# Stopping VectorE more often for GpSimd's gathers in a graph kernel that sorts neighbours

## The chip, the cores and the metric

The kernel runs on one core of one Trainium2 chip. The metric is the time of one execution on the device, in microseconds (us). A core has five engines that run their own instruction queues at the same time: TensorE (PE in the profile, PEld for its weight loads), VectorE (DVE), ScalarE (ACT), GpSimd (POOL) and SyncE (SP, which here issues plain DMA transfers). They wait for one another through semaphores. Each queue is executed in the order in which it was written.

## What is computed

There are 16 graphs of 1024 nodes; a node has 64 features. Two layers follow one another, each with a residual and a layer norm. The first removes a part of the edges, takes for each node and feature a weighted sum of three quantiles over the neighbours that remain, and puts that through a small network. The second multiplies the adjacency with the features and applies another small network. Cut to what matters:

```python
x, adj, nodemask          # (16, 1024, 64), (16, 1024, 1024), (16, 1024)

def layer_0(x, adj, mask, W1, b1, W2, b2):
    adj_d = dilate(adj, mask)          # drops every skip-th neighbour, symmetrically
    agg = 0                            # per node and feature, over its neighbours:
    for tau, wt in zip([0.25, 0.5, 0.75], [0.25, 0.5, 0.25]):
        agg += wt * quantile(sorted neighbours, tau)   # linear interpolation
    h = relu((x + agg) @ W1 + b1)
    return (h @ W2 + b2) * mask[..., None]

def layer_1(x, adj, W1, b1, W2, b2):
    messages = einsum('bij,bjh->bih', adj, x)
    return tanh(concatenate([x, messages]) @ W1 + b1) @ W2 + b2

x = layernorm(x + layer_0(x, adj, nodemask, ...))
x = layernorm(x + layer_1(x, adj, ...))
```

The edge part of the second layer does not enter the result.

## The kernel before

The 16 graphs are worked through in nine groups: one graph, seven times two graphs, and one graph (`sizes`). For each graph three kinds of work follow one another.

*Finding* (`find`, from line 495) reads the adjacency, transposes it on TensorE (`nb`, `p_nb`, `nb_t`, lines 545 to 549), counts and ranks the neighbours (`p_cnt`, `p_m`, `s`, `p_rank`, `gone`, lines 564 to 602), applies the removal (`p_stay`, `valid`, line 625), orders the nodes by their number of neighbours (`kinds`, `low`, `places`, `p_srt`, `x_q`) and writes for every node a list of its neighbours' numbers (`word`, `bits`, `codes`, `index`). At each step ScalarE or VectorE takes TensorE's result out of PSUM.

*Gathering and sorting.* The ordered nodes lie in tiles of 128. A group of two graphs has 16 tiles, worked through in eight pairs (`group.pairs`); a group of one has four pairs. For a pair, `gather` issues one indirect DMA for each position of the list (line 876): it fetches for 128 nodes one neighbour's 64 features[...]. A tile of a pair, `g`, holds as many cells of 64 columns as there are positions, twice over. Four such buffers form a ring (`RING`): the fifth pair can be gathered when the first is sorted and added up. `sort` then orders each feature's neighbours with a network of minima and maxima. Each step is a `compare`: one VectorE tensor_tensor on one or more cells of `g` (their places given by a box of start, two steps and two counts), with 64 columns a cell. All of VectorE's instructions that go through the helper `Counted` stand in the profile under line 443. When a list is sorted, `weigh` has ScalarE multiply the wanted cells in place by their weights (line 907), and `add_up` has TensorE add them (`p_agg`, lines 924 and 928), after which the buffer is free.

*Closing* (`close`) returns the sums to the nodes' own order (`back`, `parts`, `p_g`, line 965), runs both small networks and layer norms (`p_h`, `p_y`, `p_x`, `p_adj`, `p_msg`, `p_z`, `p_d`), and writes the result.

The order of all this is fixed when the program is written. `Counted` keeps an account of VectorE's time in estimated microseconds (`vector.now`). The steps of finding and closing (`Steps`) have due times on that account, and before each compare the function `around` issues those that are due. So VectorE's queue is a mixture of compares and of steps of other graphs, and each step holds up the compares behind it until its input is there.

*Stops.* `Counted` also keeps a due time for a stop. Before an instruction with two tensor inputs, if the due time has passed, it issues a `tensor_reduce` of two columns into `pause` (line 437), an instruction with one input whose result nobody uses. It reads two columns of the cell that the fourth compare back wrote (`vector.written`), and the next stop is due 1.32 us later (`GATHER`). An instruction that has not two tensor inputs and reaches the due time moves it on in the same way.

Of the kernel before, what the change touches and what calls it, by code (L numbers as in the profile page):

```python
# [17 lines left out]
ALU = mybir.AluOpType  # L18
AX = mybir.AxisListType
# [96 lines left out]
@lru_cache(None)  # L116
def network(n, least):

    def step(layer, at, way):
        at, lows, highs = dict(at), [], []
        for i, j, low, high in layer:
            ci, cj = i + n * at[i], j + n * at[j]
            at[i] ^= low and way != "high"
            at[j] ^= high and way != "low"
            oi, oj = i + n * at[i], j + n * at[j]
            if low:
                lows.append((ci, cj, oi))  # L130
            if high:
                highs.append((ci, cj, oj))
        pair = [(ALU.min, lows), (ALU.max, highs)]
        done = []
        for op, vectors in pair[::-1] if way == "high" else pair:
            done += [(op, box) for box in boxes(tuple(sorted(vectors)))] if vectors else []
        return done, at

    states = [(0, {k: 0 for k in range(n)}, [])]
    for layer in layers_of(n, least):  # L140
        found = {}
        for _, at, done in states:
            for way in ("both", "low", "high"):
                more, to = step(layer, at, way)
                key = tuple(to.values())
                if key not in found or len(found[key][2]) > len(done) + len(more):
                    found[key] = (len(done) + len(more), to, done + more)
        states = sorted(found.values(), key=lambda s: s[0])[:12]
    places = needed(n, least)
    ends = [(s[0] + len(boxes(tuple((k + n * s[1][k], i) for i, k in enumerate(places)))), j)  # L150
            for j, s in enumerate(states)]
    _, at, done = states[min(ends)[1]]
    found = [k + n * at[k] for k in places]
    return done, boxes(tuple((c, i) for i, c in enumerate(found))), found
# [3 lines left out]
def kernel(  # L158
# [15 lines left out]
    nc = tc.nc  # L174
    B, N, C = x.shape
# [201 lines left out]
    for t in range(NT):  # L377
# [5 lines left out]
                             ap=[in_block.ap[0], [NT + 1, NT]]), 1.0)  # L383
# [12 lines left out]
    CLOSING, CLOSING_LAST = 0.8, 60.0  # L396
    TURNING = 40.0
    RING = 4
    GATHER = 1.32
    pause = const.tile([P, 1], F32, name="pause")  # L400

    def block(t):
# [5 lines left out]
    class Counted:  # L408
# [9 lines left out]
        def __getattr__(self, name):  # L418
            def size_of(x):
                n = 1  # L420
                for step, size in x.ap[1:]:
                    n *= size
                return n

            def issue(out, *args, **more):
                inputs = [a for a in args if isinstance(a, bass.AP)]
                n = max([size_of(out)] + [size_of(a) for a in inputs])
                each, more_us = 0.00104, 0.0
                if name in ("tensor_scalar", "tensor_copy"):
                    each = 0.00032 if out.dtype in (BF16, F16) and inputs[0].dtype in (BF16, F16) else 0.00053  # L430
                if name == "match_replace" or "accum_out" in more:
                    more_us = 0.07
                us = 0.067 + more_us + n * each
                two = name in ("tensor_tensor", "tensor_add", "tensor_sub", "tensor_mul",
                               "scalar_tensor_tensor")
                if two and self.now >= self.due and len(self.written) >= 4:
                    nc.vector.tensor_reduce(pause, self.written[-4], AX.X, ALU.max)  # L437
                    self.due = self.now + GATHER
                    self.now += 0.065
                elif not two and self.now + us >= self.due:  # L440
                    self.due = max(self.now, self.due) + GATHER
                self.now += us
                return getattr(nc.vector, name)(out, *args, **more)  # L443
            return issue

    vector = Counted()
# [381 lines left out]
            to.add(0.2, weigh)  # L828
        return to

    def cells(g, box, which, width):

        start, (d1, n1), (d2, n2) = box
        return bass.AP(tensor=g.tensor, offset=g.offset + start[which] * width,
                       ap=[g.ap[0], [d2[which] * width, n2], [d1[which] * width, n1], [1, width]])

    def few(G):

# [56 lines left out]
    def sort(group, k, g):  # L895

        tile_k, (u, v) = TILES[group.G][k], divmod(k, group.G)
        steps, _, where = network(*tile_k)
        todo = []

        def compare(op, box):
            vector.tensor_tensor(cells(g, box, 2, C), cells(g, box, 0, C), cells(g, box, 1, C),
                                    op=op)
            vector.written = vector.written[-3:] + [g[:, box[0][2], :2]]

        def weigh(cell, place):
            nc.scalar.mul(g[:, cell], g[:, cell], group.weights[:, v, u, place:place + 1])  # L907

        for op, box in steps:
            todo.append((compare, (op, box)))  # L910
        return todo, [(weigh, (cell, place)) for place, cell in enumerate(where)]
# [452 lines left out]
    with (  # L1364
# [25 lines left out]
        with tc.For_i(0, C, 1) as c:  # L1390
# [21 lines left out]
            for t in range(NT):  # L1412
                for h in range(2):
# [3 lines left out]
                    for k in range(NT):  # L1417
                        nc.tensor.matmul(p[:, :HALF], val_t[:, k, t * P:(t + 1) * P],
                                         before[:, k, js].rearrange("p q j -> p (q j)"),
                                         start=(k == 0), stop=(k == NT - 1))  # L1420
                    w = dense.tile([P, HALF], F32, name="w", bufs=2)
# [49 lines left out]
```

## Time and profile before

| | us |
|---|---|
| median of three runs | 3934.4 |
| lowest and highest of the three | 3887.4, 4052.7 |
| profiled execution | 3815.4 |
| its span | 3813.7 |
| VectorE busy / GpSimd busy / TensorE busy | 2329.5 / 2104.7 / 1942.5 |

The profile is of one execution, and all parts below are parts of its span. In a row of the costliest groups stand the line, the engine, the operation, the tiles written and read, and the number of instructions; after the first bar the time that they were busy and the mean of one in nanoseconds; after the second the idle time of the engine just before them, and what ended most of it. VectorE's instructions overlap by some 80 ns, so their busy times add up to more than the time that they take. "issue" is time in which an engine waited for nothing that the profile shows. A timeline row begins with the start and the duration in us. A row of the stage table has the stretch, its length, the busy time of PE, PEld, DVE, ACT and POOL, each with its number of instructions, the granted TensorE clock, the DMA share and GB/s. TensorE's clock was granted at 0.709 of full speed on average.

### The profile page before, as it was taken

The numbers are of one execution on the slowest core, as the hardware profiler recorded it, in microseconds if no ns is written. First come the engines' busy times: TensorE is split into PE (matmuls) and PEld (weight loads), VectorE is DVE, ScalarE is ACT, GpSimd is POOL, SyncE is SP. The second block draws the span as 40 slices with busy tenths as digits, with TensorE's granted clock in tenths as the row PEclk, the third lists the DMA queues.
The fourth block names the chain that finished last, engine by engine and source line by source line (L and its number), as shares of the span: only waits on it lengthen the run. The fifth ranks groups of instructions, "written<-read, shape, count | busy, mean of one in ns | idle before, by whom it ended". The sixth has DMA issues, their size and how long they took to land.

```text
span 3813.7 us, 37663 instructions
## 1 busy us (share of the span) xinstructions
PE 1942.5 (51%) x10312; PEld 1070.0 (28%) x10312; DVE 2329.5 (61%) x9225; ACT 1324.3 (35%) x2945; POOL 2104.7 (55%) x1943
## 2 busy tenths in 40 slices
PE   5206523731565442963439635674336645674376
PEld 3103312420333221532224323332113323242133
DVE  4208624991598635885268844877248765768653
ACT  3204423431443332542325323544224334134123
POOL 1760346077654766167572677447571576757750
PEclk9556756765788666875669756786667866777578
DMA  2101111121212201222022212032021321242111
GB/s 99 20 19 48 58 50 32 65 52 24 64 44 87 66 18 62 82 66 43 17 67 93 67 30 65 23 105 64 18 66 28 94 58 26 60 117 62 20 47 29
DMA packets 268306, 205.67 MB, mean 54 GB/s; under 512 B 92634, under 2 KB 225290, under 8 KB 268086
## 3 DMA queue, kind: packets, MB, share of 16 engines
q1 hardware_dynamic: 207382, 147.10, 12.1%
q0 software_dynamic: 59744, 55.90, 7.5%
q8 instruction: 83, 1.36, 0.2%
q14 instruction: 137, 1.12, 0.1%
q10 hardware_dynamic: 960, 0.18, 0.0%
HBM read 203.97 MB, written 4.19 MB: 55 GB/s over the span
## 4 chain that ended last, share of the span: by engine, by line
PE 30%; another core or an unknown queue 25%; DVE 22%; ACT 9%; issue 8%; POOL 4%; DMA 1%; SPq 0%; ACTq 0%; DVEq 0%; POOLq 0%
DVE g L443 12%; PE p_msg L1144 5%; POOL g L876 4%; PE p_srt L687 3%; PE p_g L965 3%; PE p_adj L1135 2%; PE p_rank L596 2%; PE p_rank L593 2%; PE p_agg L924 2%; PE p_cnt L564 1%; PE p_nb L545 1%; ACT nb_t L549 1%; ACT g L907 1%; DVE codes L443 1%
## 5 line engine op out<-in xcount | busy, mean ns | idle before, releaser
L876 POOL DMA_INDIRECT g<-in_x_dram,index x1859 | 2075.7, 1117 | 1470.3 <-issue 560.1
L443 DVE TENSOR_TENSOR g<-g 128x128 f32<-128x128 f32 (+7 forms) x4982 | 1581.3, 373 | 199.7 <-remote 93.7
L545 PE MATMUL p_nb<-ident_h,nb 128*128 128x128 bf16 x1024 | 107.9, 280 | 649.6 <-DVE nb L443 261.9
L437 DVE TENSOR_REDUCE pause<-g 128x1 f32<-128x2 f32 x1021 | 148.5, 145 | 272.2 <-ACT g L907 240.5
L907 ACT ACTIVATE g<-g,weights 128x64 f32<-128x64 f32 x1006 | 260.0, 338 | 102.7 <-DVE g L443 84.3
L965 PE MATMUL p_g<-back,parts 128*64 128x512 bf16 x720 | 197.9, 425 | 186.6 <-DVE back L443 138.5
L443 DVE TENSOR_SCALAR gone<-gone,s 128x1024 bf16<-128x1024 f16 x128 | 64.3, 503 | 362.8 <-ACT gone L598 222.8
L598 ACT ACTIVATE gone<-p_rank,s 128x1024 f16<-128x1024 f32 x128 | 141.5, 1112 | 402.2 <-remote 303.2
L545 PEld LDWEIGHTS <-nb 128*128 128x128 bf16 x1024 | 92.6, 130 | 670.4 <-issue 489.9
L1144 PE MATMUL p_msg<-adj_t,x 128*64 128x512 f32 x416 | 232.3, 661 | 65.9 <-issue 30.4
L593 PE MATMUL p_rank<-after,blocks 8*128 8x512 bf16 x256 | 121.4, 474 | 282.0 <-ACT gone L598 147.5
L549 ACT ACTIVATE nb_t<-p_nb 128x1024 bf16<-128x1024 bf16 x124 | 122.1, 1023 | 375.0 <-remote 247.9
L924 PE MATMUL p_agg<-g,ident 128*128 128x128 f32 x918 | 161.6, 332 | 131.3 <-ACT g L907 83.7
L687 PE MATMUL p_srt<-pay,perm 128*128 128x323 bf16 x1024 | 187.0, 320 | 52.0 <-DVE x_q L443 29.4
L625 ACT ACTIVATE valid<-p_stay 128x1024 bf16<-128x1024 f32 x128 | 130.4, 1019 | 173.5 <-remote 95.0
L924 PEld LDWEIGHTS p_agg<-g,ident 128*128 128x128 f32 x918 | 143.0, 236 | 151.9 <-ACT g L907 96.4
L1137 ACT COPY adj_t<-p_adj 128x512 f32<-128x512 f32 x208 | 117.4, 584 | 162.6 <-PE p_adj L1135 79.0
L596 PEld LDWEIGHTS <-nb_t 128*128 128x128 bf16 x1024 | 70.6, 111 | 365.1 <-issue 365.1
L618 PE MATMUL p_stay<-nb,ident_h 128*128 128x512 bf16 x256 | 115.1, 450 | 105.8 <-ACT valid L625 56.3
L965 PEld LDWEIGHTS <-parts 128*64 128x64 bf16 x720 | 80.0, 119 | 280.1 <-issue 178.8
L517 ACT ACTIVATE nb<-a 128x1024 bf16<-128x1024 f32 x124 | 125.4, 1051 | 67.2 <-remote 27.1
L1135 PE MATMUL p_adj<-ident,a_block 128*128 128x128 f32 x832 | 138.6, 300 | 14.3 <-ACT z_t L1156 11.6
(188 smaller groups left out, 3054.9 us busy)
## 6 DMA issues: line engine op xcount, KB each, us to landing
a<-in_adj_dram SPq DMA_DIRECT2D x64, 1024.0 KB
a_block<-in_adj_dram SPq DMA_DIRECT2D x208, 256.0 KB
g<-in_x_dram,index POOLq DMA_INDIRECT x1859
a_ahead<-in_adj_dram SPq DMA_DIRECT2D x48, 256.0 KB
x_f<-in_x_dram SPq DMA_DIRECT2D x16, 256.0 KB
out_dram<-o SPq DMA_DIRECT2D x16, 256.0 KB
x_c<-in_x_dram SPq DMA_DIRECT2D x15, 256.0 KB
few<-index SPq DMA_DIRECT2D x45, 0.0 KB
```

The lines of the kernel that those rows point to most:

```text
L437: nc.vector.tensor_reduce(pause, self.written[-4], AX.X, ALU.max)
L443: return getattr(nc.vector, name)(out, *args, **more)
L545: nc.tensor.transpose(p[:, t], v["nb"][:, t, block(j)], ident_h)
L549: nc.scalar.activation(v["nb_t"][:, j], p.rearrange("p t c -> p (t c)"), AF.Relu)
L593: nc.tensor.matmul(p[:, half_of(h)], v["blocks"][:, block(t)], after[:, half_of(h)], start=True, stop=False, skip_group_check=True)
L687: nc.tensor.matmul(p[:, k, :PAY], v["perm"][:, t, block(2 * at + k)], pay[:, t], start=(t == 0), stop=False, skip_group_check=True)
L876: nc.gpsimd.indirect_dma_start(out=part[:, j, :], out_offset=None, in_=x_rows, in_offset=bass.IndirectOffsetOnAxis(ap=group.index[:, v, sl ...
L907: nc.scalar.mul(g[:, cell], g[:, cell], group.weights[:, v, u, place:place + 1])
L924: nc.tensor.matmul(p, ident, it, start=(k == 0), stop=(k == most - 1), skip_group_check=True)
L965: nc.tensor.matmul(v["p_g"][h][:C, :HALF], v["parts"][:, k, q], m[:, half_of(h)], start=(k == 0 and v["start"]), stop=(k == 2 and q == v[" ...
L1135: nc.tensor.transpose(p[:, block(t)], m[:, t], ident)
L1144: nc.tensor.matmul(v["p_msg"][C:2 * C, :HALF], v["x1"][:, j, :], adj_t, start=(j == 0), stop=(j == NT - 1))
```

## The change

Three things change, all in the stops and the compares.

1. The interval of the stops becomes 0.44 us (`STOP`) instead of 1.32 us.
2. A compare is split by columns where a stop falls due within it: the first part has as many columns as fit before the due time (an even number), and the next part begins with a stop. Neither part may be shorter than 0.1 us by the account (`SPLIT`); otherwise the compare stays whole.
3. `written` holds the buffer and the cell of up to eight compares. When `weigh` begins on a list, that list's entries are taken out, so that a stop reads no cell that ScalarE multiplies. A stop reads the fourth entry from the end, or the oldest if there are fewer; with none there is no stop.

```diff
-    GATHER = 1.32
+    STOP = 0.44
+    SPLIT = 0.1
...
-                if two and self.now >= self.due and len(self.written) >= 4:
-                    nc.vector.tensor_reduce(pause, self.written[-4], AX.X, ALU.max)
-                    self.due = self.now + GATHER
+                if two and self.now >= self.due and self.written:
+                    g, cell = self.written[-4:][0]
+                    nc.vector.tensor_reduce(pause, g[:, cell, :2], AX.X, ALU.max)
+                    self.due = self.now + STOP
                     self.now += 0.065
                 elif not two and self.now + us >= self.due:
-                    self.due = max(self.now, self.due) + GATHER
+                    self.due = max(self.now, self.due) + STOP
...
-    def cells(g, box, which, width):
+    def cells(g, box, which, width, columns):
 
         start, (d1, n1), (d2, n2) = box
-        return bass.AP(tensor=g.tensor, offset=g.offset + start[which] * width,
-                       ap=[g.ap[0], [d2[which] * width, n2], [d1[which] * width, n1], [1, width]])
+        return bass.AP(tensor=g.tensor, offset=g.offset + start[which] * width + columns.start,
+                       ap=[g.ap[0], [d2[which] * width, n2], [d1[which] * width, n1],
+                           [1, columns.stop - columns.start]])
...
         def compare(op, box):
-            vector.tensor_tensor(cells(g, box, 2, C), cells(g, box, 0, C), cells(g, box, 1, C),
-                                    op=op)
-            vector.written = vector.written[-3:] + [g[:, box[0][2], :2]]
+
+            us = 0.00104 * C * box[1][1] * box[2][1]
+            done = 0
+            while done < C:
+
+                due = vector.due if vector.now < vector.due else vector.now + 0.065 + STOP
+                many = 2 * int(C * (due - vector.now - 0.067) / us / 2 + 0.5)
+                to = C if many * us / C < SPLIT or (C - done - many) * us / C < SPLIT else done + many
+                vector.tensor_tensor(*[cells(g, box, which, C, slice(done, to)) for which in (2, 0, 1)],
+                                     op=op)
+                done = to
+            vector.written = vector.written[-7:] + [(g, box[0][2])]
 
         def weigh(cell, place):
+            vector.written = [w for w in vector.written if w[0] is not g]
             nc.scalar.mul(g[:, cell], g[:, cell], group.weights[:, v, u, place:place + 1])
```

## The prediction

> **What bounds the kernel now.** I read the page first (busy shares, the chain that ended last, the costliest groups), then the groups kept apart by shape, the waits of VectorE's stops, timelines of a few microseconds, and the stage table.
>
> ```profile
> PE 1942.5 (51%) x10312; PEld 1070.0 (28%) x10312; DVE 2329.5 (61%) x9225; ACT 1324.3 (35%) x2945; POOL 2104.7 (55%) x1943
> ...
> PE 30%; another core or an unknown queue 25%; DVE 22%; ACT 9%; issue 8%; POOL 4%; DMA 1%; SPq 0%; ACTq 0%; DVEq 0%; POOLq 0%
> DVE g L443 12%; PE p_msg L1144 5%; POOL g L876 4%; PE p_srt L687 3%; PE p_g L965 3%; PE p_adj L1135 2%; PE p_rank L596 2%; PE p_rank L593 2%; PE p_agg L924 2%; PE p_cnt L564 1%; PE p_nb L545 1%; ACT nb_t L549 1%; ACT g L907 1%; DVE codes L443 1%
> ...
> L876 POOL DMA_INDIRECT g<-in_x_dram,index x1859 | 2075.7, 1117 | 1470.3 <-issue 560.1
> ...
> L437 DVE TENSOR_REDUCE pause<-g 128x1 f32<-128x2 f32 x1021 | 148.5, 145 | 272.2 <-ACT g L907 240.5
> ```
>
> No engine is full. Of the chain, compares (DVE g) hold 12% and gathers (POOL g) only 4%. The 25% of "another core or an unknown queue" is neither: one core runs. Its long pieces are ScalarE waiting for TensorE answers. Two such waits from the timeline, ScalarE alone:
>
> ```profile
> 918.46 1.02 ACT L549 ACTIVATE nb_t<-p_nb 128x1024 bf16<-128x1024 bf16 x1 [17.88 <-remote]
> 940.87 1.02 ACT L549 ACTIVATE nb_t<-p_nb 128x1024 bf16<-128x1024 bf16 x1 [21.38 <-remote]
> ```
>
> Eight transposes of about 1 us together are answered 18 and 21 us late. All through this stretch gathers run one per 1.30 us with no break and VectorE is nearly idle; where VectorE is full and gathers come 1.5 us apart, such delays are under 4 us. I do not know the mechanism; I use the pattern.
>
> The stage table shows how a group of two graphs (here 2126 to 2606 us) is made up; each busy time is followed by its count:
>
> ```profile
> 2126.00:2206.00 80.00, 51.23 (x227) 26.19 (x225) 70.15 (x274) 32.82 (x99) 55.51 (x47) 0.80 0.27 71
> 2206.00:2348.00 142.00, 66.42 (x344) 40.55 (x345) 57.54 (x225) 47.76 (x113) 104.85 (x96) 0.59 0.17 39
> 2348.00:2505.00 157.00, 102.69 (x632) 57.79 (x632) 120.86 (x474) 63.82 (x127) 70.86 (x61) 0.78 0.23 73
> ```
>
> The third number is VectorE. In the first and last stage it leads, in the middle one it waits for late answers. Gathers are early for the sorts there: pair 0 of the group that sorts from 2348 us had landed by 2291 us. GpSimd, done with four pairs, then waits for a free buffer (p_agg L928, 331.4 us in 7 waits over the run).
>
> **What the change adds to VectorE.** The order of the built program counts 1021 stops before and 2818 after; compare instructions go from 4982 to 5278; all other VectorE instructions, GpSimd's gathers and SyncE's DMAs keep their numbers. A stop's price is the time from its start to the next start:
>
> ```profile
> 1095.88 3.71 DVE L443 TENSOR_TENSOR g<-g 128x384 f32<-128x384 f32 x12
> 1096.35 4.12 POOL L876 DMA_INDIRECT g<-in_x_dram,index  x1 [0.30 <-issue]
> ...
> 1100.10 0.14 DVE L437 TENSOR_REDUCE pause<-g 128x1 f32<-128x2 f32 x1
> 1100.16 0.28 DVE L443 TENSOR_TENSOR g<-g 128x128 f32<-128x128 f32 x1
> ```
>
> It is 0.065 us here (median over all 1021), so 1797 more cost 116 us. A split costs the fixed part of a compare: two of 64 columns instead of one of 128.
>
> ```profile
> L443 DVE TENSOR_TENSOR g<-g 128x128 f32<-128x128 f32 x1091 | 284.1, 283 | 59.3 <-remote 41.2 <-DVE g L443 15.4 <-issue 2.7
> ...
> L443 DVE TENSOR_TENSOR g<-g 128x64 f32<-128x64 f32 x1207 | 232.6, 216 | 11.2 <-DVE g L443 7.3 <-issue 2.9 <-DVE pause L437 0.7
> ```
>
> 67 ns per 64 columns and 135 ns start to start for 64 leave 68 ns fixed; 296 splits make 20 us. Together 136 us, or 11% on compares that take 1192 us start to start. How much is on the path? Compares hold 12% of the chain, 458 us, 38% of their 1192: 0.38 x 136 = 52 us. The stage table says the same from another side: nine groups of 15 us each, a third of which falls in the waiting stage. I take +55 us, bounds +20 and +136. The cover is the waits for ScalarE and TensorE inside the interleaved steps; without it all 136 us show.
>
> **What stops buy.** Behind twelve compares without an opening, the gather above took 4.12 us instead of 0.997. Over the trace 664 of 1859 gathers took over 1.03 us, 224 us of excess, and 331 of them ended 935 to 965 ns after a stop's start: a gather needs one opening near its beginning, and then runs through whatever VectorE does. With a stop due every 0.44 us a full VectorE opens within about 0.5 us instead of the present median of 1.56 us between stops, so I halve the excess: 112 us of GpSimd time. Its share on the path is small: POOL and DMA hold 5% of the chain, 190 us of 2652 us of gathering (7%), so 8 us. To it comes the tail (3123 to 3566 us), where gathers run nearly without a wait and the last group's sort waits for them (30.2 us, one wait): half of some 25 us of excess there. I take -15 us, bounds 0 and -112.
>
> Here the Trainium skill speaks against the change twice (SBUF — State Buffer, section "Who interferes with whom"). It says that the two engines' shared port is an exclusive lock held for a whole instruction, the loser blocking fully, and it infers that a two-input compare takes only the read side and leaves descriptor writing free. By the inference stops buy nothing: the gain is 0 and the sum rises by 15. By the lock a compare issued after a stop would wait out the gather, up to 0.95 us for each of 2818 stops. The trace differs from both: the 4.12 us gather was held by compares, and the compare at 1100.16 started 0.065 us after its stop, with the gather still running. I follow the rows.
>
> **What no stop waits for any more.** 240.5 us of stops waiting for ScalarE's multiplications, 22 waits:
>
> ```profile
>   ACT g L907: 240.5, 22
> ```
>
> That is the row of line 437. One of these waits in VectorE's timeline:
>
> ```profile
> 2175.92 2.97 DVE L443 TENSOR_TENSOR g<-g 128x64 f32<-128x64 f32 x9
> 2184.32 0.15 DVE L437 TENSOR_REDUCE pause<-g 128x1 f32<-128x2 f32 x1 [5.44 <-ACT g L907]
> ```
>
> They fall in two kinds. Thirteen of 2 to 9 us stand in full compare stretches, as here, with 4 to 84 us of ready work behind them: together 73 us, of which I credit 45, because the next wait (1.2 us at 2205, then 8.61 us for p_d at 2229) takes up a part. The long ones (74.05 us at 954, 33.4 at 1904, 16.1, 13.9, 12.9) are followed by only 1 to 4 us of work and then by the graph search's own wait (s for p_m at 957.8; low for valid at 2343), late next in their place. I credit 5 us. Sum -50 us, bounds 0 and -240. The stop that remains reads a compare made up to four earlier, at times the last one: 39.2 us in 54 waits of VectorE for itself bounds that at +10 us, by its nearest row; a gain is excluded, since a wait only adds. I take 0.
>
> **Order.** Each sort counts as longer in the planner, so search and closing steps come earlier, by about 0.5% of all compare columns, about 6 us. With them moves every DMA they issue: GpSimd's queue keeps its order, but on SyncE's the loads of `few` and `a_block` change places here and there. In the timeline at 861 us SyncE takes 0.58 to 0.84 us to issue one such DMA, so a set of twenty put ahead of an `a_block` load delays it by some 14 us, or frees it by as much; GpSimd waits for `few_x`, TensorE's p_adj and ScalarE behind it for `a_block`. Both ways, I take 0, with 15 us a group at the very most.
>
> Sum: 55 - 15 - 50 = -10 us on 3813.7 us of span (3815.4 us with what lies around it): 0.3%, which is nothing. The profiled execution was 119 us below the median of three, 3934.4 us; from that median I predict **3930 us**.
>
> **Rivals.**
> *Slower: TensorE answers later.* Stretched gathers may be what lets TensorE through: with stops, gathers in full stretches come nearer to 1.35 us apart instead of 1.5 to 1.6, and the late answers of the middle stage start some 20 us earlier in each group. At about 5 us an answer and three answers a group that waits on them, eight groups give +120 us, and with the stop cost uncovered (+80 over my 55) +200: 4040 to 4130 us. For it: answers 10 us late already at 1.38 us spacing (2604 to 2632 us). Against it: in full stretches at 1.43 us there were none. It decides if the spacing in full stretches falls under about 1.4 us.
> *Faster: the stops' waits were the path.* If the 73 us count in full, 50 of the long 167 us as well, and half of the halved gather excess (56 us), the sum is 55 - 73 - 50 - 56 = -124 us: 3810 us. For it: the search's transposes wait for VectorE's nb (261.9 us in 9 waits), which lies behind those stretches. Against: the short work behind the long waits.
> *It doesn't do what it says:* the first compare of a pair finds no cell to stop on, and stops where no gather runs buy nothing. The cost stays, the gain goes: +55 - 50 = 3940 us, which is no change either.
>
> **How the numbers follow.** Flat, with the third rival, 0.45; slower 0.30; faster 0.25. Two per cent, 79 us, is about what a measurement of this kernel can tell from no change, its runs being 3887 to 4053. Of the flat case 0.05 spills over each bound, of each rival 0.05 falls short of its own: faster 0.25, same 0.45, slower 0.30. The flat case alone spans 3870 to 4010 us; the range 3820 to 4070 leaves out a tenth on either side.
>
> **What would show it.** Right: some 2800 stops at 145 ns with next to no wait for ACT g; gathers with a mean under 1.07 us instead of 1.117; compares busy about 70 us longer in records; the idle time moved to s, gone, low and x_q waits. Wrong: the unknown share of the chain well above or below 25%; gathers still over 1.1 us; p_agg waits of GpSimd far under 331 us.

## The result, and the profile after

The changed kernel takes 4107.9 us in the median of four runs (4086.5 to 4111.8), the kernel before 3951.7 us in the median of its four beside it. The ratio is 1.049, with a 95% interval of 1.037 to 1.062: slower. Ratios here and below are formed from the runs of each kernel that lie within 1.5% of its fastest, while the medians are of all its runs, so a ratio can be larger than that of the two medians (here 1.040). The profiled execution has a span of 4103.6 us, 290 us more than the profiled one of before, which was itself 136 us under its median.

From the page of the changed kernel: the busy time, the chain by engine and by line, and the groups of gathers, compares and stops.

```profile
PE 1955.9 (48%) x10276; PEld 1064.1 (26%) x10312; DVE 2460.0 (60%) x11318; ACT 1331.1 (32%) x2945; POOL 2048.5 (50%) x1943
...
DVE 28%; PE 26%; another core or an unknown queue 24%; issue 10%; ACT 7%; POOL 3%; DMA 2%; SPq 0%; ACTq 0%; DVEq 0%; POOLq 0%
...
L879 POOL DMA_INDIRECT g<-in_x_dram,index x1859 | 2021.7, 1087 | 1636.6 <-issue 598.1
L445 DVE TENSOR_TENSOR g<-g 128x128 f32<-128x128 f32 (+11 forms) x5278 | 1688.6, 358 | 115.3 <-remote 49.8
L439 DVE TENSOR_REDUCE pause<-g 128x1 f32<-128x2 f32 x2818 | 409.5, 145 | 92.5 <-remote 54.7
```

The counts are those that the order gave: 2818 stops and 5278 compares. No stop's wait for ScalarE leads its row any more, and a gather takes 1087 ns instead of 1117. VectorE has 130 us more busy time, but its span has grown by 290 us: span less busy time was 1484 us and is 1644 us. So VectorE does not only work longer, it waits longer. Four of its longest waits (engine, line, releaser: us in total, times, longest), before and then changed:

```profile
DVE gone L443 <- ACT gone L598: 222.8, 73, 27.6
DVE s L443 <- PE p_m L571: 102.4, 9, 41.8
DVE x_q L443 <- ACT srt L691: 92.8, 34, 30.8
DVE low L443 <- ACT valid L625: 39.1, 6, 15.6
```

```profile
DVE gone L445 <- ACT gone L600: 253.5, 95, 26.8
DVE s L445 <- remote: 200.2, 5, 65.7
DVE x_q L445 <- issue: 158.7, 15, 37.9
DVE low L445 <- ACT valid L627: 148.0, 9, 37.1
```

All are steps of the finding whose input goes back to TensorE. The idle time did go to s, gone, low and x_q, but it grew on the way.

The chain that ended last, by line, before and changed:

```profile
by line: another core or an unknown queue 24.6%; DVE g L443 11.7%; issue 8.3%; PE p_msg L1144 4.8%; POOL g L876 4.2%; PE p_srt L687 3.2%; PE p_g L965 3.0%; PE p_adj L1135 2.1%; PE p_rank L596 1.9%; PE p_rank L593 1.8%; PE p_agg L924 1.8%; P
by line: another core or an unknown queue 23.8%; DVE g L445 16.3%; issue 9.7%; PE p_msg L1157 4.3%; PE p_srt L689 3.1%; POOL g L879 2.7%; DVE pause L439 2.4%; PE p_g L978 2.3%; PE p_rank L598 2.1%; PE p_rank L595 2.0%; PE p_agg L937 1.7%; P
```

The share of "another core or an unknown queue", the untold share below, is 938 us before and 977 us after, so it grew by 39 of the 290 us. Compares (DVE g) went from 446 to 669 us, and stops (DVE pause) hold 98 us. None of the prediction's three signs of being wrong appeared: the untold share stayed near 25%, a gather stayed under 1.1 us in the mean, and GpSimd's waits for p_agg, 331.4 us at line 928 before, are 350.7 us at the same line (now 941).

Where in a group does the time lie? I take the start of the first gather of each of the eight pairs, and the distance to the next pair's, in us, as a mean over the five groups from the third to the seventh:

```
pair                        0     1     2      3     4     5     6     7    sum
before                   73.7  53.7  48.5  115.2  61.8  37.1  30.2  26.5  446.8
changed                  77.8  58.8  48.0  103.0  98.8  36.9  32.4  26.8  482.6
```

In the pairs 5 to 7, where the stops are densest (139 of a group's 350 in 96 us), 2.3 us a group are lost. In the pairs 0 to 4, where finding and closing are interleaved, it is 33.5 us. But 24.8 us of that lie in pairs 3 and 4, which hold another 154 stops in 202 us, and of the 179 us of the five groups 105 fall in a single one (423 us before, 528 changed). So this table alone does not tell stops from interleaved steps.

### The profile page after: what moved, and what is told of

The parts are those of the page before. It is cut to its first block, busy times and chain, and to the rows that moved or that the text cites. A ratio compares the mean times of both kernels' runs of the same rounds, so it can differ in the third digit from the quotient of the medians.

```text
span 4103.6 us, 39632 instructions
## 1 busy us (share of the span) xinstructions
PE 1955.9 (48%) x10276; PEld 1064.1 (26%) x10312; DVE 2460.0 (60%) x11318; ACT 1331.1 (32%) x2945; POOL 2048.5 (50%) x1943
## 4 chain that ended last, share of the span: by engine, by line
DVE 28%; PE 26%; another core or an unknown queue 24%; issue 10%; ACT 7%; POOL 3%; DMA 2%; SPq 0%; ACTq 0%; DVEq 0%; POOLq 0%
DVE g L445 16%; PE p_msg L1157 4%; PE p_srt L689 3%; POOL g L879 3%; DVE pause L439 2%; PE p_g L978 2%; PE p_rank L598 2%; PE p_rank L595 2%; PE p_agg L937 2%; PE p_adj L1148 2%; ACT nb_t L551 1%; PE p_stay L625 1%; PE p_nb L547 1%; PE p_stay L620 1%
## 5 line engine op out<-in xcount | busy, mean ns | idle before, releaser
L879 POOL DMA_INDIRECT g<-in_x_dram,index x1859 | 2021.7, 1087 | 1636.6 <-issue 598.1
L445 DVE TENSOR_TENSOR g<-g 128x128 f32<-128x128 f32 (+11 forms) x5278 | 1688.6, 358 | 115.3 <-remote 49.8
L439 DVE TENSOR_REDUCE pause<-g 128x1 f32<-128x2 f32 x2818 | 409.5, 145 | 92.5 <-remote 54.7
L595 PE MATMUL p_rank<-after,blocks 8*128 8x512 bf16 x256 | 130.9, 511 | 362.4 <-ACT gone L600 178.1
L445 DVE TENSOR_REDUCE x_q<-p_srt 128x128 f32<-128x384 f32 x64 | 35.6, 556 | 226.2 <-issue 158.7
L620 PE MATMUL p_stay<-nb,ident_h 128*128 128x512 bf16 x236 | 101.0, 428 | 124.7 <-ACT valid L627 77.2
```

Of the source, the lines that this page charges most:

```text
L439: nc.vector.tensor_reduce(pause, g[:, cell, :2], AX.X, ALU.max)
L595: nc.tensor.matmul(p[:, half_of(h)], v["blocks"][:, block(t)], after[:, half_of(h)], start=True, stop=False, skip_group_check=True)
L879: nc.gpsimd.indirect_dma_start(out=part[:, j, :], out_offset=None, in_=x_rows, in_offset=bass.IndirectOffsetOnAxis(ap=group.index[:, v, sl ...
```

## Experiments

The theories: **VectorE pays in full** (136 us of stops and splits, with nothing to cover them); **TensorE answers later** (the prediction's slower rival); **the waiting only moves** (part 3 lets VectorE run on to the next wait); **order** (the planner's shifted account); and the prediction's own sum. "Late" below counts ScalarE's waits that end over 1 us after the last matmul before them has ended; before has 110 of them with 931.7 us, the changed kernel 113 with 1176.1 us. This counts a wait from the last matmul on, also while ScalarE had other work. How much it rises depends on the count: ScalarE's idle time that the profile puts down to "remote" is 972 us in 101 waits before and 1066 us in 98 after. Below, "late" is given as this idle time. Before's only profile is of an execution 136 us under the median, so its 972 us may be low.

### The parts singly, on a device where no answer is late

*Part 3 alone* (label e1_no_wait; interval 1.32, no splits):

```diff
-                if two and self.now >= self.due and len(self.written) >= 4:
-                    nc.vector.tensor_reduce(pause, self.written[-4], AX.X, ALU.max)
+                if two and self.now >= self.due and self.written:
+                    g, cell = self.written[-4:][0]
+                    nc.vector.tensor_reduce(pause, g[:, cell, :2], AX.X, ALU.max)
...
+            vector.written = [w for w in vector.written if w[0] is not g]
```

> The kernel before with the third part of the change alone: stops every 1.32 us as before, no splits, but a stop never reads a tile that ScalarE multiplies. The prediction's third step: the 240.5 us of VectorE waiting for ScalarE go, 50 us of it come off the time: ratio to the kernel before 0.985 to 0.99. Theory 'VectorE pays in full' (stops and splits cost what they take): same 0.98 to 1.00. Theory 'the waiting only moves' (VectorE runs past and then waits for ScalarE's products elsewhere, TensorE later): 1.00 to 1.03, with the waits for ScalarE turning up again under gone, low and x_q.

*Stops alone* (e2_often):

```diff
-    GATHER = 1.32
+    GATHER = 0.44
```

> The kernel before with the stop interval 0.44 instead of 1.32 and nothing else: about 2800 stops, no splits, stops still read cells that ScalarE multiplies. Theory 'VectorE pays in full': 1800 stops by 0.065 us is 117 us, all on the path, plus waits for ScalarE: ratio 1.03 to 1.05. Theory 'TensorE answers later': ScalarE's late answers rise from 932 us towards 1176 us as in the changed kernel and the ratio is 1.04 to 1.06 whatever VectorE's share. Theory 'order' (the planner's shifted account) expects the full loss too, 1.03 to 1.05; 'the waiting only moves' expects 1.00 to 1.02, since its part is not made here.

*The changed kernel without splits* (e3_no_split):

```diff
-    SPLIT = 0.1
+    SPLIT = 1000.0
```

> The changed kernel without splits of the compares: 296 fewer instructions, a stop comes only between whole compares. 'VectorE pays in full': 20 us less than the changed kernel, and somewhat fewer stops (each 0.065 us): ratio to the kernel before 1.03 to 1.045. 'TensorE answers later', 'order', 'the waiting only moves': no change from the changed kernel, 1.04 to 1.06. If splits delay the order of the sort's steps more than their price, the ratio falls under 1.03.

*The changed kernel with every third stop* (e4_third; account, order and splits stay):

```diff
-                    nc.vector.tensor_reduce(pause, g[:, cell, :2], AX.X, ALU.max)
+                    self.stops += 1
+                    if self.stops % 3 == 0:
+                        nc.vector.tensor_reduce(pause, g[:, cell, :2], AX.X, ALU.max)
```

> The changed kernel with its splits, its account and its order, but only every third stop issued (about 940). 'VectorE pays in full': 1879 stops by 0.065 us is 122 us less: ratio to the kernel before 1.01 to 1.025. 'TensorE answers later because the openings let the gathers run unbroken': late answers fall back to about 930 us and the ratio is 0.99 to 1.01. 'Order' or 'the waiting only moves': the stops are not the cause and the ratio stays at 1.04 to 1.06.

Measured: before took 3018.6 us here, 933 us less than beside the result. Ratios: part 3 alone 0.998 (0.996 to 0.999), stops alone 1.042 (1.040 to 1.045), without splits 0.9965 (0.9948 to 0.9982), every third stop 1.019 (1.017 to 1.021). In none of the four traces does ScalarE or VectorE have a single wait put down to "remote"; before's profile has 972 and 209 us of them. What is missing has the size of the late answers: 931.7 us in before's profile, in an execution that stood 797 us above this median. This device doesn't have them.

"VectorE pays in full" falls here: three times the stops, beside part 3, cost nothing (0.9965 against 0.998), and leaving two of three away makes the kernel slower (1.019, against 1.005 for the changed kernel on such a device, further down). Where the stops' time comes from stands in VectorE's waits, first with part 3 alone, then with part 3 and all stops:

```profile
DVE g L444 <- DMA g<-in_x_dram,index: 379.0, 17, 47.2
```

```profile
DVE g L445 <- DMA g<-in_x_dram,index: 260.6, 12, 42.5
```

Compares wait for their gathers 118 us less; 1705 more stops by 0.065 us are 111 us, and VectorE's idle time falls from 704.5 to 592.0 us. The stops are paid with time that VectorE spent waiting for gathers.

Stops alone cost 127 us because they still read cells that ScalarE multiplies. Their waits, VectorE's and then GpSimd's, in that kernel:

```profile
DVE pause L437 <- ACT g L907: 92.1, 22, 11.8
```

```profile
POOL g L876 <- PE p_agg L924: 87.5, 6, 21.0
...
POOL g L876 <- PE p_agg L928: 45.7, 2, 45.0
```

VectorE stands 92 us at stops, and GpSimd waits 133 us for a buffer that TensorE has not yet added up; with part 3 as well these last waits are 15.4 and 34.7 us. So part 3, worth little alone, is what lets the stops be frequent.

### The changed kernel again, and part 3 with splits

> The changed kernel itself, again. In the four runs above no answer of TensorE was late at all, and the kernel before took 3019 us there instead of 3952: exactly the 932 us of late answers were missing. Theory 'TensorE answers later': the 1.049 belonged to the late answers (931.7 to 1176.1 us in the two profiles); where none is late the ratio is 1.00 to 1.02, where they occur again it is 1.04 to 1.06. Theory 'VectorE pays in full': 1.03 to 1.045 in either case, since 136 us are added to VectorE.

Part 3 with splits and no more stops (e9_rare) is the changed kernel with this:

```diff
-    STOP = 0.44
+    STOP = 1.32
```

> The changed kernel with the interval back at 1.32: part 3 and splits, but no more stops than before. Where no answer of TensorE is late: 'splits are what costs' (the run with a third of the stops and all splits stood at 1.019, the one with all stops and no splits at 0.9965) expects 1.01 to 1.025; 'only the planner's order differs' expects anything between 0.99 and 1.02, not tied to the splits' number; the prediction's price of splits (68 ns each) expects 1.00. Where answers are late again, 'TensorE answers later' expects about the kernel before, 0.99 to 1.01.

These two fell on a device with late answers: before 3951.4 us, the changed kernel 4085.0 us, ratio 1.045 (1.031 to 1.059), 1038 us late; part 3 with splits 4136.7 us, 1.059 (1.046 to 1.072), 966 us late, which is no more than before's 972. With the stops as rare as before the loss is no smaller. The stops are not needed for it. Nor are more late answers: in this kernel's chain the untold share is 23.5% of 4083.7 us, 960 us, and the compares hold 10.8%, 441 us, both about as before.

### Part 3 again, splits alone, and a spacing of the gathers

> Part 3 alone once more, for a device on which TensorE's answers are late (there the changed kernel stood at 1.045 and part 3 with splits but without more stops at 1.059; without late answers part 3 alone stood at 0.998). 'Part 3 is what makes TensorE late' (VectorE no longer held by ScalarE runs ahead, is done sooner, and the sort's and the finding's TensorE work falls into gathers with an idle VectorE): 1.03 to 1.06. 'The splits and the order they make are the cause': 0.98 to 1.01. The prediction's step: 0.987. If no answer is late in this run: 0.998 again.

*Splits alone* (e10_splits): the split `compare`, with interval 1.32 and the old reading of cells.

```diff
-            vector.tensor_tensor(cells(g, box, 2, C), cells(g, box, 0, C), cells(g, box, 1, C),
-                                    op=op)
+            while done < C:
...
+                vector.tensor_tensor(*[cells(g, box, which, C, slice(done, to)) for which in (2, 0, 1)],
+                                     op=op)
+                done = to
```

> The kernel before with the splits alone: stops every 1.32 us with the old reading of cells, compares split where such a stop is due. 'Splits are what costs where no answer is late' (1.019 in the run with all splits and a third of the stops): 1.01 to 1.025. The prediction's price (some 220 splits by 68 ns, 15 us of VectorE): 1.00. Where answers are late: 'the splits are the cause' 1.04 to 1.06, 'part 3 is the cause' 0.99 to 1.01.

*Spacing* (e8_pace): before, with a memset ahead of each gather.

```diff
                 slot_no = first[u] + j - 1
+                nc.gpsimd.memset(spaced, 0.0)
                 nc.gpsimd.indirect_dma_start(
```

> The kernel before with a GpSimd memset of a spare 128x16 tile ahead of every gather, nothing else changed; the gathers then come some 0.1 to 0.3 us further apart than 1.30 us. 'The unbroken pace of the gathers holds TensorE's answers up': where answers are late, the 932 us of them shrink by half or more and the ratio is 0.85 to 0.97. 'The pace is not what matters': late answers stay and the ratio is 1.02 to 1.08, since 1859 memsets of about 0.15 us lengthen GpSimd by 280 us. Where no answer is late: 1.02 to 1.08, GpSimd's own price.

No answer was late here (before 3020.2 us). Part 3 alone: 0.996 (0.993 to 0.998), as before. Splits alone: 1.011 (1.009 to 1.013), 33 us by the ratio, though its 202 splits by the prediction's 68 ns are 14 us of VectorE. The spacing: 1.066, and it tested nothing. Its memsets in the trace (count: shortest, median and longest ns, first and last start in us):

```profile
L877 POOL MEMSET spaced<- x1859: 101/112/618, 14.4 to 741.5; 128x16 f32 x186
```

The last starts at 741.5 us of 3224. Nothing in the kernel ties a memset to its gather by data, and they all ran ahead, in the first two groups; the gathers of the later groups kept their pace.

### The changed kernel on a device without late answers, and a stop of another kind

> The changed kernel a third time. Two devices so far (7 runs) showed no late answer of TensorE, one (the first result and 2 runs) showed them in every run. Where none is late: 'TensorE answers later' as the whole cause expects 0.99 to 1.01; 'splits cost 1 to 2 per cent, and the stops nothing' (splits alone 1.011, splits with a third of the stops 1.019, all stops without splits 0.9965) expects 1.01 to 1.025; 'VectorE pays in full' expects 1.03 to 1.045. Where answers are late: 1.045 again.

*Two-input stops* (e6_closed): two of three stops become this.

```diff
+                        nc.vector.tensor_tensor(closed, g[:, cell, :2], g[:, cell, :2], op=ALU.max)
```

> The changed kernel with two of three stops replaced by a two-input maximum of the same two columns into a spare tile: VectorE's time and order stay, only the openings for GpSimd go. If openings are worth what the prediction said (112 us of GpSimd, 15 on the path), where no answer is late it is 0 to 1% slower than the changed kernel, 1.02 to 1.035; 'VectorE pays in full' expects no difference from the changed kernel, 0.122 ms of VectorE above the run with a third of the stops (1.019), so 1.055; 'stops cost nothing on the path' expects 1.02 as in that run.

On a third device without late answers (before 3020.2 us) the changed kernel takes 3034.8 us: 1.005 (1.003 to 1.008). From its page:

```profile
PE 1868.3 (62%) x10312; PEld 1028.0 (34%) x10312; DVE 2441.6 (80%) x11318; ACT 1323.3 (44%) x2945; POOL 2179.0 (72%) x1943
...
DVE 36%; PE 24%; POOL 19%; issue 7%; DMA 6%; ACT 6%; SPq 1%; ACTq 0%; DVEq 0%; POOLq 0%
...
L879 POOL DMA_INDIRECT g<-in_x_dram,index x1859 | 2149.9, 1156 | 729.3 <-issue 515.6
```

It is the same program with nearly the same busy times, in 1070 us less. "Another core or an unknown queue", 24% above, is gone from the chain. Four steps of the ranking in the first group, in ScalarE's timeline, show what it was; first beside the result, then here:

```profile
148.39 1.11 ACT L600 ACTIVATE gone<-p_rank,s 128x1024 f16<-128x1024 f32 x1 [21.30 <-remote]
173.61 1.11 ACT L600 ACTIVATE gone<-p_rank,s 128x1024 f16<-128x1024 f32 x1 [24.11 <-remote]
201.66 1.11 ACT L600 ACTIVATE gone<-p_rank,s 128x1024 f16<-128x1024 f32 x1 [26.94 <-remote]
229.67 1.11 ACT L600 ACTIVATE gone<-p_rank,s 128x1024 f16<-128x1024 f32 x1 [26.89 <-remote]
```

```profile
125.28 1.11 ACT L600 ACTIVATE gone<-p_rank,s 128x1024 f16<-128x1024 f32 x1 [0.54 <-PE p_rank L598]
127.43 1.11 ACT L600 ACTIVATE gone<-p_rank,s 128x1024 f16<-128x1024 f32 x1 [1.03 <-PE p_rank L598]
129.57 1.11 ACT L600 ACTIVATE gone<-p_rank,s 128x1024 f16<-128x1024 f32 x1 [1.03 <-PE p_rank L598]
131.72 1.11 ACT L600 ACTIVATE gone<-p_rank,s 128x1024 f16<-128x1024 f32 x1 [1.03 <-PE p_rank L598]
```

Four steps 2.15 us apart on the one device, 25 to 28 us apart on the other. The gathers beside them do not differ. The stage table between such steps, in the same order (the third of the busy times is VectorE's, the fifth GpSimd's):

```profile
155.00:160.00 5.00, 0.00 (x0) 0.00 (x0) 0.00 (x0) 0.00 (x0) 3.88 (x4) 0.50 0.11 26
160.00:165.00 5.00, 0.00 (x0) 0.00 (x0) 0.00 (x0) 0.00 (x0) 3.78 (x5) 0.50 0.10 26
```

```profile
125.00:130.00 5.00, 5.00 (x24) 1.86 (x22) 0.00 (x0) 2.66 (x3) 3.78 (x5) 0.50 0.12 26
130.00:135.00 5.00, 4.90 (x24) 2.17 (x23) 0.00 (x0) 2.92 (x3) 3.78 (x5) 0.50 0.06 11
```

Four or five gathers in 5 us, an idle VectorE and a granted clock of 0.50 in both; TensorE works in the second and stands still in the first. So none of the three is enough to make TensorE late: they are the setting, and something else decides. What is known of it is that it goes with the set of runs, each made on one device.

With two-input stops the ratio is 1.010 (1.008 to 1.013), 0.5% above the changed kernel and 0.9% below every third stop alone. The mean gather is 1156 ns with all stops, 1164 with two-input ones in their place, 1212 with a third of them.

### Spacing once more, and other intervals

> The kernel before with the memset of a spare 128x16 tile ahead of every gather from the third group on only (1337 or so of 1859 gathers; in the run with it everywhere, the first two groups lost 170 us and the others kept their 343 us). Where no answer of TensorE is late: 0.995 to 1.01, these groups have room for it. Where answers are late: 'the unbroken pace of the gathers, with nothing between two of them, holds TensorE's answers up' expects the groups' periods to fall from about 450 us towards 345 and a ratio of 0.80 to 0.95; 'the pace is not what matters' 0.99 to 1.03.

> Part 3 and stops every 0.66 us, no splits (every 0.44 us without splits stood at 0.9965, every 1.32 us at 0.997, where no answer is late). Where none is late: 0.99 to 1.00 by every theory. Where answers are late, this is the changed kernel without its splits: 'the splits and the order they make bring the 4.9%' expects 0.99 to 1.01; 'part 3 lets VectorE finish sooner and leaves TensorE's work beside gathers and an idle VectorE' expects 1.03 to 1.06; the prediction's sum 0.99 to 1.00.

> Part 3 alone with half as many stops, every 2.64 us. Where no answer is late: if stops are worth nothing on the path, 0.99 to 1.00; if the openings matter, gathers grow past 1.2 us each and the ratio is 1.01 to 1.03. Where answers are late: 'part 3 is the cause' 1.03 to 1.06; 'the splits are the cause' 0.98 to 1.01.

The edits are the memset under `if group.number > 1:`, `STOP = 0.66` with `SPLIT = 1000.0`, and part 3 alone with `GATHER = 2.64`. A fourth device without late answers (before 3020.9 us). The spacing: 1.045, with all memsets again in front (1499 of them; the first group's period is 317 us, with part 3 alone 210), so once more no test. Two thirds as many stops without splits: 1.005 (1.003 to 1.006), 0.8% above every 0.44 us and 0.7% above every 1.32 us; such a step up and down with the interval is not explained by any price of a stop. Half as many stops as before: 1.041 (1.037 to 1.044). Its gathers, and VectorE's wait for them:

```profile
L877 POOL DMA_INDIRECT g<-in_x_dram,index x1859 | 2359.7, 1269 | 675.4 <-issue 515.0
```

```profile
DVE g L444 <- DMA g<-in_x_dram,index: 500.5, 30, 46.7
```

Mean gathers of 1269, 1181 and 1152 ns at intervals of 2.64, 1.32 and 0.44 us: the first step was worth 164 us of GpSimd and about 130 us of time (4.3% against part 3 alone), the second 54 us of GpSimd and no time that can be told.

### The parts singly, where answers are late

> Part 3 alone a third time (0.998 and 0.996 on two devices without late answers). On a device with late answers: 'part 3 is the cause of the 4.5 to 5.9% there' 1.03 to 1.06; 'the splits and the order they make are the cause' 0.98 to 1.01.

> The changed kernel without splits again (0.9965 on a device without late answers). On a device with late answers: 'part 3 is the cause' 1.03 to 1.06, as in the changed kernel (1.045) and in part 3 with splits (1.059); 'the splits and the order they make are the cause' 0.98 to 1.01; VectorE's price of the stops, if it shows there alone, 1.02 to 1.03.

> The stops alone again (1.042 on a device without late answers, where VectorE waited 92 us for ScalarE at the stops). On a device with late answers the parts so far: part 3 alone 1.023, part 3 and stops 1.034, part 3 and splits 1.059, all three 1.045 to 1.049. 'Part 3 is the cause there' expects only the stops' own price, 1.01 to 1.045; 'each part that shifts the order makes the answers later' 1.03 to 1.06; if the stops hold VectorE for ScalarE longer there, 1.06 to 1.10.

> The splits alone again (1.011 on a device without late answers). On a device with late answers: 'part 3 is the cause there' 1.00 to 1.015; 'each part that shifts the order makes the answers later' 1.02 to 1.05.

Two devices, both with late answers: before 3957.3 us for the first two, 3959.0 us for the others. With them all ratios by part; for late answers the interval, the ratio of the two medians, and ScalarE's late time (before 972 us in its one profile):

| | no answer late | answers late | of medians | late, us |
|---|---|---|---|---|
| part 3 | 0.998, 0.996 | 1.023 (1.004 to 1.042) | 1.008 | 1114 |
| splits | 1.011 | 1.009 (1.004 to 1.014) | 1.013 | 974 |
| stops | 1.042 | 1.036 (1.021 to 1.050) | 1.028 | 996 |
| part 3, stops | 0.9965 | 1.034 (1.019 to 1.048) | 1.020 | 1036 |
| part 3, splits | not run | 1.059 (1.046 to 1.072) | 1.047 | 966 |
| all three | 1.005 | 1.045 (1.031 to 1.059), 1.049 (1.037 to 1.062) | 1.034, 1.040 | 1038, 1066 |

Of these seven only the last is a difference of over 2% beyond doubt; the splits alone are under it, and for the others it stays unclear. Part 3 alone shows the most late time, and the largest untold share of the chain, 1173 us of 3975.4:

```profile
by line: another core or an unknown queue 29.5%; DVE g L444 10.6%; issue 9.4%; PE p_msg L1146 4.7%; POOL g L877 2.6%; PE p_srt L688 2.6%; PE p_g L967 2.3%; PE p_adj L1137 2.1%; PE p_rank L597 2.0%; PE p_rank L594 1.9%; PE p_agg L926 1.6%; A
```

With splits, stops, or part 3 and splits, late time is hardly above before's. "Part 3 is the cause" as the only one falls with the stops (1.036 without it), "the splits are the cause" with part 3 and stops, and "each part makes the answers later" with this last column. The parts may not add up either: part 3 with splits loses more (1.059) than the two alone multiply to (1.032), though the intervals touch. On these devices every edit came out slower, by little for part 3 and splits; on the others part 3 gains a little and repairs the stops.

## Why the prediction was wrong

**The stops' and splits' cost** (+55 us on the path). Counts and price held: 2818 stops, start to next start 0.065 us in the median. The compares' records grew by 107 us, not 70. What lies on the path was divided wrongly. Where no answer is late, 111 us of stops beside part 3 cost nothing, since the compares wait that much less for gathers, and 296 splits with the 95 stops that come with them cost 27 us (1.005 against 0.9965), which is about the prediction's own price, 20 and 6. Splits alone cost 33 us for 202 of them, and why was not found. The stated cover, waits for ScalarE and TensorE, was not the one that paid. The cross-check by stages did not say the same either: of nine times 15 us, a third under cover leaves 90 us, not 55. Where answers are late, the changed kernel's chain runs through 223 us more of compares, but with the stops as rare as before through no more of them, at no smaller a loss; so the share of the chain does not give the price.

**What stops buy** (-15 us). The excess of gathers over 0.997 us fell from 224 to 170 us, so by 54 and not 112: in the full stretches (20 us with VectorE over 95% busy) gathers are still some 1.55 us apart, as before. "Mean under 1.07 us" was missed at 1087 ns. In the prediction's example the opening was not the stop: the gather ended at 1100.47 us, 0.37 us after the stop began and 0.88 us after the last compare had ended at 1099.59, so a break in VectorE's work opened it. The terms, 8 us and half of 25, also gave 20 and not 15. As to time, the value is in the first stops: from 2.64 to 1.32 us some 130 us, from there on nothing. The inference of the Trainium skill (SBUF — State Buffer, section "Who interferes with whom"), that two-input compares leave descriptor writing free, would have made them worth nothing at any interval; the measurement decides against it.

**No stop waits for ScalarE** (-50 us, at most 0). This is the step that failed first. The waits went, as forecast, but the time did not. Part 3 alone brings 7 to 12 us where no answer is late. Where answers are late it loses 2.3% (0.4 to 4.2%), some 90 us by the ratio and 34 by the medians, and so lies outside its bounds. The 240.5 us on which the step rested were largely made by the late answers: with splits alone, stops wait 44.6 us for ScalarE on a device without them and 308.0 us on one with them. Without these waits VectorE stood idle longer, 1652 us against 1484, and the untold share of the chain is 1173 us against 938 (before's execution having been a short one). This is what the theory "the waiting only moves" expected, on these devices.

**Order** (0, at most 15 us a group, both ways), and with it the late answers, which the sum carried over unchanged. This failed with it: a wait of 932 us, a quarter of the span, was called unexplained and then held constant, without a reason. Where no answer is late, the whole change came to +0.5%, against the predicted -0.3%. Where they are late it came to +4.5 and +4.9% by the ratio, and to 134 and 156 us by the medians. Part 3's 2.3% is about half of that. The rest, some 2.2 to 2.6%, comes with stops and splits, for which the sum had 55 - 15 = 40 us or 1%; with intervals of 1.4 to 1.9% on each ratio that excess is not certain. That a changed order is what makes part 3 lose is argued, not shown.

**The rival** "TensorE answers later" gave 4040 to 4130 us, and the time fell there, by luck in the main. Its sign did not come: the pace in the full stretches did not fall under 1.4 us. Of its 120 us of later answers ScalarE's idle time shows 94 and the chain 39.

What stays open: why TensorE's answers are late on some devices, and whether the gathers' unbroken pace is needed for it, since both attempts at spacing them failed to space them. Each of the seven sets of runs behind the result was made on a device of its own, so device and set cannot be told apart. What carries the loss of part 3 with splits, whose late answers and compares are as before, is open too. No run changed the order alone.

No version run on both kinds of device beats the kernel before on both. Part 3 with all stops and no splits gains 0.35% on the one and loses 3.4% on the other.

## What to carry to other kernels

When a quarter of the critical chain goes to a wait that has no cause in the program, measure the kernel on a second device before pricing a change, and do not hold that wait constant: here it tells a 0.5% loss from a 4.9% one. Price an inserted instruction by what the engine was waiting for at that place: stops that fall into a wait for the gathers they speed up are free, and the first of them are worth far more than the last. An instruction inserted to space others should be tied to them by data: without that, all 1859 memsets here ran in the first 741.5 us.

## What was not expected of the hardware

- The same program takes 3019 to 3021 us in the median on four devices and 3951 to 3959 us in the four sets with late answers, with no run in between (the highest without is 3037 us; the lowest with is 3885, and the profiled execution of before took 3815). The executions without late answers lie within 1%, those with them within 4.5%, the profiled one left out.
- The late answers end on a grid of their own. Three such waits of ScalarE in before's profile end exactly 28.00 us apart:

```profile
189.71 1.11 ACT L598 ACTIVATE gone<-p_rank,s 128x1024 f16<-128x1024 f32 x1 [26.89 <-remote]
217.71 1.11 ACT L598 ACTIVATE gone<-p_rank,s 128x1024 f16<-128x1024 f32 x1 [26.89 <-remote]
245.71 1.11 ACT L598 ACTIVATE gone<-p_rank,s 128x1024 f16<-128x1024 f32 x1 [26.89 <-remote]
```

In the eight traces with late answers, 57 to 74% of the distances of 0.35 to 30 us between the ends of "remote" waits of ScalarE and VectorE lie within 0.1 us of a multiple of 0.70 us, where chance gives 29%. For multiples of the gathers' 1.30 us it is 6 to 16%, and chance gives 15%. So the ends do not follow the pace of the gathers. What sets the 0.70 us is not known.
- A two-input maximum of two columns serves a gather almost as well as the one-input stop. With two-input ones for two of three, 323 of 969 gathers over 1.03 us ended 935 to 965 ns after such an instruction's start, and 208 after a stop; the row of the former:

```profile
L445 DVE TENSOR_TENSOR closed<-g 128x2 f32<-128x2 f32 x1879 | 290.2, 154 | 0.0
```

That 0.5% of time separates the two kinds leaves some advantage to the one-input stop, but an opening is not tied to having one input. What the two share is their two columns; no run tried a longer one.
